# A gated recurrence rebuilt from seven block products instead of eight, in blocks of 512 positions

## The chip, the cores and the metric

One core of a Trainium2 chip runs the kernel. The core has a matrix engine (PE, whose weight loads the profile lists as PEld), a vector engine (DVE), a scalar engine (ACT), a general one (POOL), and a queue that issues transfers (SP). They run side by side and wait for each other through semaphores. SBUF is the on-chip memory that all of them read; PSUM holds the sums of PE in eight banks of 128 partitions by 512 float32 columns; DRAM is reached by transfers. The metric is the time of one execution in microseconds. Three executions of the kernel before took 2949.99, 2952.07 and 2953.89 us, so the median is 2952.07.

## The reference

The input r has 8 sequences of 2048 positions and 512 channels. Two layers follow one another, each with a normalisation before it, a normalisation of its result and a residual sum:

```
x = r
x = x + layernorm(gelu(longconv(layernorm(x))))          # a state-space convolution along the 2048 positions
n = layernorm(x)
for the 8 steps t (the batch axis is the time of this layer; the 2048 positions are its batch):
    f = sigmoid(n[t] @ wf.T + c @ uf.T + bf)
    i = sigmoid(n[t] @ wi.T + c @ ui.T + bi)
    g = tanh   (n[t] @ wc.T + c @ uc.T + bc)
    c = f * c + i * g                                    # c starts from in_c in every position
h = tanh(n @ wo.T + c_final @ uo.T + bo)                 # n[t] for each t, c_final once
x = x + layernorm(h)
```

All the 512 x 512 matrices and all rows of n and c are float32. The kernel splits each operand into a float16 value and a float16 remainder and adds three float16 products, so each product of the reference is three on PE.

## The kernel before

The first stage computes the convolution kernel and the statistics of the input rows. The second stage is the convolution itself, in 16 groups of 32 channels (loop over `g`, lines 601 to 659, `NG` = 16). Within a group, 16 slots (`s_`) each issue matmuls for this group (`conv_mm`), the state chain of the next group (`chain_hi`, `chain_lo`, `chain_in`, `tap_step`), and the normalisation of the group after that (`norm_x`). The last group is `conv_last` (line 545): it first finishes the first `JF` = 2 blocks of 128 positions, so that the next stage can begin, and then the others. The result goes to DRAM as `y_d`. The gate weights are loaded and split into halves during groups 1, 2, 13 and 14 and stay in SBUF.

The third stage is the gated recurrence, over eight blocks (`q`) of 256 positions and eight steps `t`. For each (q, t):

- `prep` (line 687) loads rows of `y_d` and of r, normalises (`lnstat`: DVE's statistics, POOL's power -1/2), adds, and writes x1 to DRAM for the end; `norm` normalises again; `turn` (line 712) transposes on PE and splits into halves `xt`. These run two steps ahead (`AHEAD`).
- `scan` (line 725) takes four output blocks `m` of 128 channels. For each it issues 3 gates x 4 input blocks x 3 products of 128x128 by 128x256 for x, and as many for the state `ch` where t > 0, into PSUM tiles `pfi` and `pgg`. ACT applies tanh (line 744), DVE forms the new state (lines 750 to 754), ACT and DVE split it (755, 756).
- `head` (line 776) computes the x part of the output for the block before (q-1), 24 products with 512 columns, adds the state's part `uo` (from `last`, line 766), applies tanh, normalises and adds x1, which it reads back. Its last sum is on POOL (line 792). The heads of the last block come after all scans.

The order on PE, ACT, DVE and POOL is the order of the program text in the stretches under `manual_schedule`, and a scheduler's elsewhere; the order on SP is always the scheduler's. A tile pool with `bufs=n` hands the same memory out again when its earlier user is done, and the wait for that is inserted for the new user. The helper `mm3` (line 386) issues the three products; in the profile all products that go through it have its lines 388 to 390 and are told apart by their tiles.

## Time and profile before

The profiled execution took 2954.2 us; its span, from the first to the last instruction, is 2952.4 us.

| | us |
|---|---|
| median of three executions | 2952.07 |
| profiled execution | 2954.2 |
| its span | 2952.4 |
| PE busy | 2828.6 |
| DVE busy | 1670.6 |
| ACT busy | 1017.7 |
| POOL busy | 718.5 |
| last product of the convolution starts | 610.1 |
| first product of the recurrence starts | 616.5 |
| last gate product of the recurrence starts | 2891.1 |
| mean granted clock of PE | 0.979 |

A group line of the page names the line, engine and operation, the tile written and those read, the shape, the count, and after the bar the busy time in all, the mean of one in ns, and the idle time of the engine just before, with what ended most of it. A line of the busy time by stretch gives, after the window and its length, PE, PEld, DVE, ACT and POOL with their instruction counts, then PE's granted clock (1.00 is full), the share of the transfer engines and the rate in GB/s. A timeline line gives the start, the duration, the engine, the line and the operation. Matmuls overlap: a product of 256 columns is shown with 0.27 us, but the starts of neighbours show the pace.

### The profile page before, as it was taken

To read this page: it belongs to the slowest core of one execution; us is meant where nothing else is said; L and a number is where in the kernel's file an instruction comes from. 1 tells how busy PE (TensorE), PEld (TensorE's weight loads), DVE (VectorE), ACT (ScalarE), POOL (GpSimd) and SP (SyncE) were. 2 spreads that over 40 slices of the span, in tenths; PEclk is the share of its full clock that TensorE was granted. 3 is DMA by queue.
4 is the path that set the end of the run, shared out by engine and by line. 5 is a ranking of instruction groups with operands and counts; after the bars stand their busy time and mean duration, and the time that the engine had idled before them with its cause. 6 is when DMAs were issued, how large, how long until landed. Compare 5 with 4: busy or idle time off the path is not lost.

```text
span 2952.4 us, 59431 instructions
## 1 busy us (share of the span) xinstructions
PE 2828.6 (96%) x25044; PEld 2353.3 (80%) x25044; DVE 1670.6 (57%) x3674; ACT 1017.7 (34%) x2288; POOL 718.5 (24%) x723
## 2 busy tenths in 40 slices
PE   4679999899999999999999999999999999999998
PEld 3368888798888888888788878887888888888884
DVE  8867777647445555555555565555555655553336
ACT  8856666623222222222222222222222222222222
POOL 5757877301001111111111111111111211110003
PEclk8689999989999999999999999999999999999999
DMA  6867777747222222222222232223222322221002
GB/s 236 291 206 230 227 228 233 206 110 158 73 58 72 72 72 72 72 72 72 72 72 72 72 80 70 69 70 86 72 72 72 80 69 72 70 78 44 30 30 104
DMA packets 459476, 311.32 MB, mean 105 GB/s; under 512 B 282310, under 2 KB 377032, under 8 KB 455112
## 3 DMA queue, kind: packets, MB, share of 16 engines
q1 hardware_dynamic: 458776, 306.99, 37.4%
q8 instruction: 196, 3.21, 0.5%
q14 instruction: 72, 0.59, 0.1%
q10 hardware_dynamic: 432, 0.52, 0.1%
HBM read 206.28 MB, written 101.19 MB: 104 GB/s over the span
## 4 chain that ended last, share of the span: by engine, by line
PE 74%; issue 10%; DVE 4%; DMA 3%; POOL 3%; ACT 1%; POOLq 0%; SPq 0%; DVEq 0%; ACTq 0%
PE pfi L390 12%; PE pfi L389 12%; PE pfi L388 12%; PE pgg L389 6%; PE pgg L388 6%; PE pgg L390 6%; PE pz L390 3%; PE pz L389 3%; PE pz L388 3%; PE pt L721 2%; PE pyt L389 2%; PE pyt L390 2%; PE pyt L388 1%; DVE xg L467 1%; DMA wl<-in_wt 1%
## 5 line engine op out<-in xcount | busy, mean ns | idle before, releaser
L389 PEld LDWEIGHTS <-w 128*128 128x128 f16 x5808 | 568.1, 98 | 73.2 <-issue 6.4
L388 PEld LDWEIGHTS <-w 128*128 128x128 f16 x5808 | 568.1, 98 | 72.1 <-issue 0.7
L390 PEld LDWEIGHTS <-w 128*128 128x128 f16 x5808 | 568.0, 98 | 72.0
L388 PE MATMUL pfi<-xt,w 128*128 128x256 f16 x2048 | 559.8, 273 | 0.7 <-ACT xt L83 0.7
L389 PE MATMUL pfi<-xt,w 128*128 128x256 f16 x2048 | 560.0, 273 | 0.0
L390 PE MATMUL pfi<-xt,w 128*128 128x256 f16 x2048 | 559.8, 273 | 0.1
L388 PE MATMUL pfi<-ch,w 128*128 128x256 f16 x1792 | 488.6, 273 | 5.1 <-ACT ch L755 5.1
L390 PE MATMUL pfi<-ch,w 128*128 128x256 f16 x1792 | 488.6, 273 | 0.1
L389 PE MATMUL pfi<-ch,w 128*128 128x256 f16 x1792 | 488.6, 273 | 0.0
L744 ACT ACTIVATE gate<-pfi,bias 128x256 f32<-128x256 f32 x512 | 214.6, 470 | 656.2 <-PE pfi L390 655.7
L750 DVE SCALAR_TENSOR_TENSOR a<-gate,cd 128x256 f32<-128x256 f32 x224 | 114.9, 513 | 514.6 <-ACT gate L744 514.6
L680 POOL TENSOR_TENSOR rsh<-rsh,nhalf 128x2 f32<-128x2 f32 (+1 forms) x65 | 45.1, 694 | 1465.3 <-DVE rsh L679 1442.0
L755 ACT ACTIVATE ch<-cd 128x256 f16<-128x256 f32 x256 | 106.5, 416 | 516.5 <-DVE cd L754 516.5
L388 PE MATMUL pgg<-xt,w 128*128 128x256 f16 x1024 | 279.3, 273 | 0.0
L389 PE MATMUL pgg<-xt,w 128*128 128x256 f16 x1024 | 279.2, 273 | 0.0
L390 PE MATMUL pgg<-xt,w 128*128 128x256 f16 x1024 | 279.1, 273 | 0.0
L388 PE MATMUL pgg<-ch,w 128*128 128x256 f16 x896 | 244.4, 273 | 0.0
L389 PE MATMUL pgg<-ch,w 128*128 128x256 f16 x896 | 244.4, 273 | 0.0
L390 PE MATMUL pgg<-ch,w 128*128 128x256 f16 x896 | 244.2, 273 | 0.0
L792 POOL TENSOR_TENSOR x1r<-x1r,h 128x512 f32<-128x512 f32 x124 | 182.2, 1488 | 41.1 <-DVE h L791 41.1
L753 DVE SCALAR_TENSOR_TENSOR gate<-gate,gate 128x256 f32<-128x256 f32 x256 | 110.6, 432 | 136.8 <-ACT gate L744 136.8
L83 ACT ACTIVATE xt<-pt 128x512 f16<-128x512 f32 x128 | 75.8, 596 | 316.3 <-PE pz L390 218.3
(301 smaller groups left out, 5786.6 us busy)
## 6 DMA issues: line engine op xcount, KB each, us to landing
xs<-in_rr SPq DMA_DIRECT2D x32, 1024.0 KB, 7.1
t<-kpad SPq DMA_DIRECT2D x32, 1024.0 KB, 5.3
xr<-in_r SPq DMA_DIRECT2D x128, 256.0 KB, 3.4
x_d<-x SPq DMA_DIRECT2D x128, 256.0 KB, 3.4
x1r<-x_d SPq DMA_DIRECT2D x128, 256.0 KB, 3.2
out<-x1r SPq DMA_DIRECT2D x128, 256.0 KB, 2.0
y<-y_d SPq DMA_DIRECT2D x62, 512.0 KB, 5.5
y_d<-y SPq DMA_DIRECT2D x30, 1024.0 KB, 7.7
```

The lines of the kernel that those rows point to most:

```text
L83: S.activation(hi, src, AF.Copy)
L388: T.matmul(out, lhsT=w(0), rhs=x(0), start=start, stop=False)
L389: T.matmul(out, lhsT=w(1), rhs=x(0), start=False, stop=False)
L390: T.matmul(out, lhsT=w(0), rhs=x(1), start=False, stop=stop)
L467: V.tensor_tensor(xg, xg, bc(rs1), ALU.mult)
L680: Q.tensor_tensor(rs, rs, nhalf[:, 0:n], ALU.pow)
L721: T.transpose(pt[:, k], xn[:, k * P : (k + 1) * P], ident)
L744: S.activation(r, outs[gt], AF.Tanh, scale=gsc[gt], bias=bs[:, gt, m : m + 1])
L750: V.scalar_tensor_tensor(a2, gate[0], 1.0, cst_[q, t - 1, m], ALU.add, ALU.mult)
L753: V.scalar_tensor_tensor(gate[1], gate[1], 1.0, gate[2], ALU.add, ALU.mult)
L755: S.activation(ch[:, 0], cd, AF.Copy, scale=0.5)
L792: (V if (q, t) >= (NQB - 1, NB - 2) else Q).tensor_tensor(x1r, x1r, hv[cj], ALU.add)
```

## The change

Each 512 x 512 product is cut into 2 x 2 blocks of 256 and formed by seven block products instead of eight, with sums of blocks taken on both operands beforehand and of results afterwards. The block of positions grows from 256 to 512 (`QC` = 4 blocks of 128), so there are four blocks `q` and 32 steps (q, t).

- **Weights.** For each of seven matrices the four blocks give seven operands (three plain, four sums), in two halves each; they are formed during groups 1 to 14 of the convolution (`weight_pieces`) and kept in DRAM as `wf_d`, then loaded whole (`weights`): two matrices at group 14, one at group 15, four when the convolution is over. The first state's part of the bias is formed on DVE from `in_c` and the untransposed matrices (`first_piece`) instead of by 144 one-column products.
- **Rows.** `prep` takes two steps t at a time and writes x1 to DRAM; `turn` reads x1 back, normalises, transposes and forms the seven operands `xf`. Scaling a row (`scaled`) moves from DVE to ACT, with the negative mean formed on POOL.
- **Products.** A unit is a gate and a half `n` of its channels, or for the x part of the output ("z") a half of the positions; its sums lie in a PSUM tile `u` of four columns blocks (two banks), of which three exist. `part_x` issues four of the seven products for x, `part_c` those for the state; then ACT copies one block, DVE adds it to the others inside PSUM (line 879), and `part_b` lets the other three products add to these sums. Each step has two z units and six gate units, interleaved by hand.
- **State.** `state` forms the new state for half of the channels and its seven operands `cf`.
- **Output.** The x part goes to DRAM as `z_d`, the state's part as `u_d`, and `head` reads both back, one row block at a time, for the block before; the last 32 row blocks follow at the end. `JF` becomes 4.

```diff
-JF = 2
+JF = 4
+QC = 4
+FIRST = (((FA11, FB11, UX), (FS2, FT2, UY)), ((FS1, FT1, UV), (FS3, FT3, UZ)))
+THEN = ((FA12, FB21, UX), (FN22, FT4, UZ), (FS4, FB22, UV))
...
+    def first_piece(gt, m):
+        un = FJ.tile([P, H], F32, name="un")
+        dma(out=un, in_=a["un"][gt, m])
+        V.scalar_tensor_tensor(un, un, 1.0, c0r, ALU.mult, ALU.mult, accum_out=puc[:, gt, m : m + 1])
...
+        for n, job in enumerate(jobs):
+            if n < NG - 3:
+                at(n + 1, 0 if n == 0 else -1, job[0])
+                for s_, f in zip(JS, job[1:]):
+                    at(n + 1, s_, f)
...
+    def scaled(out, x, mu, rs):
+        nm = FE.tile([P, 1], F32, name="nm", bufs=4)
+        Q.tensor_tensor(nm, mu, rs, ALU.mult)
+        Q.tensor_scalar(nm, nm, -1.0, None, ALU.mult)
+        S.activation(out, x, AF.Identity, scale=rs, bias=nm)
+
+    def prep(q, tp, cj):
...
+            xr = xas[k] = FJ.tile([P, 2, H], F32, name="xr", tag="wl")
...
+        def sum_():
+            y, xr = ytile.pop(k), xas.pop(k)
+            for t, (mu, rs) in enumerate(xas.pop((k, 0))):
+                yv, xv = y[:, :, t], xr[:, t].rearrange("p (g h) -> p g h", h=HS)
+                scaled(yv, yv, mu, rs)
+                Q.tensor_tensor(xv, yv, xv, ALU.add)
+            dma(out=x1_d[c, :, 2 * tp : 2 * tp + 2], in_=xr)
...
+    def turn(q, t, i):
...
+        def norm():
+            for x, (mu, rs) in zip(xas[k], xas.pop((k, 0))):
+                scaled(x, x, mu, rs)
+        def split_():
...
+            S.activation(b1, pt[:, :, 0:2], AF.Copy)
+            V.tensor_tensor(ts[:, 0:2], pt[:, 1].rearrange("p (a k) c -> p a k c", a=2), b1, ALU.subtract)
+            V.tensor_tensor(ts[:, 2], pt[:, 1, 2:4], ts[:, 0], ALU.subtract)
+            V.tensor_tensor(ts[:, 3], ts[:, 2], pt[:, 0, 2:4], ALU.subtract)
+            for f, src in (...):
+                split(xf[:, f, 0, :, cs], xf[:, f, 1, :, cs], src)
...
+    def part_x(key):
+        u = units[key] = pu.tile([P, 4, BP], F32, name="u")
+        for pr in FIRST:
+            mms(u, places(key, pr), *views(key)[0], True, not key[1] or key[2] == "z")
+
+    def part_c(key):
...
+        if t and not z:
+            mms(u, FIRST[0][:1] + FIRST[1] + FIRST[0][1:], *views(key)[1], False, True)
+        if z:
+            g = zts[key] = FJ.tile([P, 4, BP], F32, name="zt", tag="ws")
...
+        S.activation(u2, u[:, UX], AF.Copy)
+        V.tensor_tensor(u2, u2, u[:, UY], ALU.add)
+        V.tensor_tensor(c22, u2, u[:, z_], ALU.add)
+        V.tensor_tensor(c22, c22, u[:, v_], ALU.add)
+        V.tensor_tensor(u[:, 2:4], u[:, 2:4], u2[:, None].to_broadcast([P, 2, BP]), ALU.add)
+        if not z:
+            S.activation(c22, c22, AF.Tanh, ...)
+
+    def part_b(key):
...
+        mms(u, places(key, THEN), *wx, False, z or not t)
+        if z:
+            zt = zts.pop(key)
+            S.activation(zt[:, 0], u[:, UX], AF.Copy)
+            S.activation(zt[:, 1:3], u[:, 2:4], AF.Copy)
+            for h in range(2):
+                dma(out=z_d[QC * q + n + 2 * h, :, t], in_=zt[:, 2 * h : 2 * h + 2].rearrange("p a b -> p (a b)"))
+            return
+        if t:
+            mms(u, THEN, *wc, False, True)
...
+        act(g[:, 0:2], u[:, 0:3:2], bs[:, n : n + 1])
+        act(g[:, 3], u[:, UZ], bs[:, n + 2 : n + 3])
+        if kind == 2:
+            V.scalar_tensor_tensor(g, gates.pop((q, t, 1, n)), 1.0, g, ALU.add, ALU.mult)
+        elif kind == 0:
+            state(q, t, n)
...
+    def head(q, cj, t0, tail=False):
...
+        def sum_():
+            (V if tail else Q).tensor_tensor(z, z, us_[c], ALU.add)
+        def gate():
+            S.activation(heads[k], heads[k], AF.Tanh, scale=1.0 / SW)
+        def stat():
+            x1r = FT.tile([P, H], F32, name="x1r", bufs=2)
+            dma(out=x1r, in_=x1_d[c, :, t0])
+            heads[k, 0] = lnstat([heads[k]], "h") + [x1r]
+        def out():
+            z, ((mu, rs), x1r) = heads.pop(k), heads.pop((k, 0))
+            scaled(z, z, mu, rs)
+            Q.tensor_tensor(x1r, x1r, z, ALU.add)
+            dma(out=a["out"][c, :, t0], in_=x1r)
...
+            keys = [(q, t, "z", 0), (q, t, "z", 1)] + [(q, t, gt, mp) for mp in range(2) for gt in (1, 2, 0)]
+            for sl, key in enumerate(keys):
+                part_x(key)
+                if sl == 3:
+                    part_b(before)
+                    before = keys[2]
+                part_c(key)
+                go(*side.get(2 * sl, ()))
+                if before and sl != 2:
+                    part_b(before)
+                if sl != 2:
+                    before = key
+                go(*side.get(2 * sl + 1, ()))
+        part_b(before)
+        go(*last(NQB - 1))
+        rows = [head(NQB - 1, cj, t, True) for cj in range(QC) for t in range(NB)]
+        D = (0, 1, 1, 1, 2)
+        for n in range(len(rows) + max(D)):
+            for st_, d in sorted(enumerate(D), key=lambda v: -v[1]):
+                if 0 <= n - d < len(rows):
+                    rows[n - d][st_]()
```

The pieces of `prep`, `turn`, `head` and `last` are put between the units by hand, at sixteen places (`side`, two to a unit): a step with heads has two preps, two turns (for the step that follows) and four head rows.

## The prediction

> **What bounds the kernel now.** Read first the busy shares and the 40 slices of the page, then the busy time by stretch, then the costliest groups with shapes kept apart, PE's timeline and the waits.
>
> ```profile
> PE 2828.6 (96%) x25044; PEld 2353.3 (80%) x25044; DVE 1670.6 (57%) x3674; ACT 1017.7 (34%) x2288; POOL 718.5 (24%) x723
> PE   4679999899999999999999999999999999999998
> DVE  8867777647445555555555565555555655553336
> ```
> ```profile
> 184.00:548.00 364.00, 344.80 (x4008) 303.95 (x4008) 270.16 (x453) 247.71 (x552) 282.90 (x232) 0.99 0.75 225
> 588.00:592.00 4.00, 4.00 (x68) 4.00 (x67) 0.72 (x5) 0.47 (x1) 0.00 (x0) 0.52 0.95 271
> 700.00:2800.00 2100.00, 2094.50 (x17759) 1745.51 (x17758) 1110.47 (x2479) 539.80 (x1164) 284.41 (x276) 1.00 0.28 72
> ```
> ```profile
> 1199.73 0.27 PE L388 MATMUL pgg<-xt,w 128*128 128x256 f16 x1
> 1199.84 0.27 PE L389 MATMUL pgg<-xt,w 128*128 128x256 f16 x1
> 1199.95 0.27 PE L390 MATMUL pgg<-xt,w 128*128 128x256 f16 x1
> ```
> ```profile
> 1203.22 0.42 ACT L755 ACTIVATE ch<-cd 128x256 f16<-128x256 f32 x1 [5.37 <-DVE cd L754]
> 1204.21 0.84 ACT L744 ACTIVATE gate<-pfi,bias 128x256 f32<-128x256 f32 x2 [0.58 <-PE pfi L390]
> ```
> ```profile
> L744 ACT ACTIVATE gate<-pfi,bias 128x256 f32<-128x256 f32 x512 | 214.6, 470 | 656.2 <-PE pfi L390 655.7
> L792 POOL TENSOR_TENSOR x1r<-x1r,h 128x512 f32<-128x512 f32 x124 | 182.2, 1488 | 41.1 <-DVE h L791 41.1
> L753 DVE SCALAR_TENSOR_TENSOR gate<-gate,gate 128x256 f32<-128x256 f32 x256 | 110.6, 432 | 136.8 <-ACT gate L744 136.8
> ...
> L83 ACT ACTIVATE xt<-pt 128x512 f16<-128x512 f32 x128 | 75.8, 596 | 316.3 <-PE pz L390 218.3
> ```
> ```profile
> x1r<-x_d SPq DMA_DIRECT2D x128, 256.0 KB, 3.2
> out<-x1r SPq DMA_DIRECT2D x128, 256.0 KB, 2.0
> ```
>
> The second line of the page shows PE at nine tenths from slice 5 to the end. In the stretches the columns are the five engines' busy time, PE's clock, the DMA share and GB/s. From 700 to 2800 us PE is busy 2094.5 of 2100; its waits there total 5.3. Matmuls start every 0.109 us: PE's count of products is the time. ACT, DVE and POOL stand waiting (ACT 656 us for PE), so their round trips cost nothing now.
>
> **The change, part by part.**
>
> *PE, saved.* Before, 512 positions at t>0 take 2 x 288 products at 0.109, 2 x 24 of 512 columns (0.216 apart in the last heads) and 16 transposes (four in 0.60): 62.8+10.4+2.4 = 75.6. After: 6 gates x 84 + 2 x 42 for the x part = 588 products, 64.1, plus 2.4: 66.5. At t=0: 44.2 before, 39.0 after. 28 x 9.1 + 4 x 5.2 = 276 us saved; the same-shaped output product of the last state gets 60 products of 512 columns per 512 positions for 48, +2.6, four times. If the other engines kept up, that would be the gain.
>
> *Side engines, added.* Per step of 512 positions (`part_x`, `part_c`, `part_b` for two z units and six gate units) they now also combine PSUM blocks, split seven operand sums, copy z, reread z and x1. ACT, DVE and POOL run in the order written by hand, so a wait for another engine holds all behind it. `scaled` is the link: POOL makes `nm` in two tiny operations, ACT scales, POOL adds, and the next row's `nm` stands behind that add.
>
> I walk one step with heads (q>=1, t>0) from the end of ACT's tanh of the unit before the last. Rows used: ACT 256 columns 0.38 copy and 0.47 tanh, 512 columns 0.60 to 0.69, 1024 1.06; DVE 256 0.42, 512 0.69, 1024 1.28, statistics of two rows 1.7; POOL add 1.45, power 0.7; a hand-over 0.04. `nm` has no row: between the 0.20 of a POOL copy of 128x5 and the 0.55 of the one-column power; I take 0.25, nearest to the copy. ACT's clock:
> - 9.0: u2 of z0, the last gate's tanh, `state` on DVE with its four copies.
> - 18.4: u2 of z1. `zt` has one buffer, so DVE's c22 of z1 waits for z0's write: copies end at 10.3, landing 2.0 to 3.4 later, I take 13.5. Behind it: z1's sums, prep's statistics (1.7), the first gate's four DVE operations, its tanh.
> - 25.9: prep's two rows and turn's two, the link at full length: scale to 19.0, POOL's add 20.6, `nm` 21.1, scale 21.8, add 23.3, power 24.1, `nm` 24.6, scale 25.3, scale 25.9. ACT works 2.5 of these 7.5 us.
> - 33.5: z1's copies, u2, DVE's sums, heads a and b (an add between them), tanh.
> - 36.8: turn's split, ACT and DVE in turns.
> - 47.4: two gates; between them DVE's 1024-column product, two statistics (3.4), sums.
> - 54.1: prep, turn again. 60.4: tanh and `state` of the first half.
> - 68.0: u2, tanh, heads' statistics, second split. 71.3: heads c and d. 74.6: last gate.
>
> PE needs 66.5 of that 74.6. Operations back to back go at a shorter pitch (two of 0.47 in 0.84 above), so I take 73 (66.5 to 79). Without heads (q=0) about 7 go: 67 (66.5 to 70). PE's places of waiting: the x products of the third gate (third `u` buffer, freed by z1's copies at 26.9) and the last gate's second half (DVE sums at the end of the step).
>
> t=0: PE needs 39, but the side work is that of other steps, plus `last` (13.0 of PE, four DVE additions through one buffer) or, at q=0, four preps: 75 (55 to 85) and 70 (60 to 80).
>
> *Lead-in.* Before: last convolution product 610.2, first scan product 616.5. After: the first rows go statistics, scale, add, DRAM, back, statistics, scale, transpose, split, twice, the second pair behind the first; `xr` has one buffer, so a row pair is loaded only after the one before has landed. Four weight loads of 1.8 MB stand before these writes on SP's queue: 7.3 MB at 271 to 291 GB/s, 26 us. By rows: weights landed 640; second pair's add 647, landed 650, back 653, split 662; second half 693. The step then runs as if begun at 685: 75 after the convolution (40 to 110).
>
> *Convolution.* Groups of 28 us gain about 4.8 us of DVE, 2.1 of ACT and 1.7 MB; DVE is at 74%, DMA at 0.75 and 225 GB/s, which becomes about 286 where the busiest slice has 291. Hidden by those gaps, or 14 x 5 us if gone: 20 (0 to 70). The 4.8 us are four sums of 256 columns (0.42 each), products of 512, 256 and 1024 (0.69, 0.42, 1.28) and one of 512 for the first state's bias; ACT's are 0.60, 0.40 and 1.06. The last group's first part takes four blocks instead of two: as many products, same time; the cover is PE's own work. 144 one-column products (5 us) go; they lie in the lead-in.
>
> *Tail.* Before, 61 us from the last scan product (2891) to the end, PE working on heads. After, 32 rows remain, PE done. First state, `last`, u through DRAM: 28 us. Then per row the loop: `nm` twice, scale 0.63, tanh 0.63, statistics 1.1, power 0.55, hand-overs: 3.6 (x1r's two buffers: write 2.0, load 2 to 3.2, add 1.4, over two, 3.5). 28 + 32 x 3.6 + 5 = 148 (133 to 165).
>
> *Sum* against the profiled run, 2954.2 us (span 2952.4; 2.1 above the median of the three runs, 2952.07): 610 + 20 + 75; q=0 70 + 7 x 67 = 539; q=1..3 3 x (75 + 7 x 73) = 1758; last half unit 3; tail 148; 2 around the span: 3155, so 3153 on the median's scale, 6.8% slower.
>
> **A rule weighed.** The rows: at 588 to 592 the clock stands at 0.52 with PE busy throughout, after a stretch of waits. The Trainium skill, TensorE: Matmul & The Clock Gate, "The HAM clock gate (the 'warmup' mystery)", says that an idle window of about 3.4 us halves the clock until a busy one passes. My walk has two PE waits near 3.7 us per step; by the rule each could cost up to 1.7 us of PE time, an estimate from that page of 71 us over 21 steps if PE were last, giving 3224. By the rows I leave it out: in the groups of 28 us PE waits too and the clock is 0.99.
>
> **Rivals.**
> (a) *PE stays last in every step* (the other side): the waits of ACT fall into time that PE fills. For: ACT is busy only 26% in the scan. Against: it is not its busy time but its hand-overs that add up. Every step at 66.5, t=0 at 55 to 60: with my lead-in and tail 2946; with their low ends and no loss in the convolution 2876. It decides only where a step with heads takes under 65 us with my other terms (2954 = 612+20+75+539+24p+151), which is below PE's own 66.5, so lead-in and tail must shrink too.
> (b) *Worse*: SP's queue holds loads behind writes that wait, or the clock halves: steps of 79, lead-in 110, convolution 70, high ends all through: 3300 to 3444. For: each step issues some 30 transfers on SP, many of them waiting for POOL; against: most have ten us and more of lead.
> (c) *The products do not get cheaper*: 0.124 apart instead of 0.109, the weight load (98 ns in the rows, hidden) coming out. PE then needs 75 per step, more than the side walk: 21 steps of 75 to 76 for 73 and seven of 75 for 67, 3250. It can be told from the forecast only in the profile. Against: shape and operands are the same as now.
>
> **How the numbers follow.** Forecast (3060 to 3260) 0.64; (a) 0.15, of it 0.08 faster, 0.01 same, 0.06 slower; (b) 0.18; (c) 0.03. Within 0.2% is about what a measurement of this kernel can't tell from no change. Faster 0.08, same 0.01, slower 0.91. The range 2970 to 3330 leaves out the better part of (a) and the worse part of (b), some 2 in 10.
>
> **What would show it.** Right: PE's slices at 8 and 9 from q=1 on, steps with heads near 73 us by the pitch of `z_d` writes and near 67 before; ACT's idle before L766 put down to POOL, DVE's before L877 to a DMA; a hole of some 75 us after the convolution; a tail of about 148 us with PE at 0. Wrong: steps at 66.5 throughout, or row tails far from 3.6 us.

## The result, and the profile of the changed kernel

The changed kernel takes 3450.43 us (median of four runs, 3449.84 to 3452.41) where the kernel before takes 2951.03 (2949.48 to 2953.89) on the same chip: 1.169 times as long, 95% interval 1.167 to 1.171. The profiled run has a span of 3448.0 us. The direction and the chief mechanism, engines that wait for each other in their fixed orders, are as forecast; the size is not: it is 297 us more than the 3153 forecast, 120 above the upper end of the range.

The stages, in us of the profiled run, beside the terms of the prediction's sum:

| stage | predicted | measured |
|---|---|---|
| up to the last convolution product | 610 + 20 | 655 |
| lead-in | 75 | 92 |
| q=0: first step, seven others | 70, 7 x 67 | 82, 7 x 74.9 |
| q=1 to 3: first step, seven others | 75, 7 x 73 | 93.4, 7 x 78.7 |
| last half unit and tail | 3 + 148 | 162 |

The steps are counted from one first write of `z_d` to the next; the tail starts at the last gate product (3286.0), and the lead-in is what is left of the span. Of q=3's seven, the last ones (t=5 and t=6, and t=7 within the rest) have no rows left to prepare and take 66.1 to 66.2; the 18 steps that have both head rows and preparation take 80.8 on average.

From the page of the changed kernel, busy shares, PE's 40 slices and the clock that PE was granted:

```profile
PE 2726.7 (79%) x23940; PEld 2298.1 (67%) x23940; DVE 2073.9 (60%) x4254; ACT 1499.4 (43%) x3020; POOL 1167.7 (34%) x1782
PE   4688888437999898788888877888888788889920
PEclk8799999668999999899999999999999899999965
```

PE is at 96% no longer. There is a hole after the convolution (the 4 and 3) and an empty end, and in between PE is at 7 to 9 tenths; no other engine is full either. Who waits for whom stands in the groups from 700 to 3280 us (busy us and mean ns, then idle time before them and its releaser):

```profile
L837 PE MATMUL u<-xf,w 128*128 128x256 f16 x8046 | 1018.3, 286 | 247.0 <-DVE u L879 232.9 <-ACT gate L900 7.0 <-DVE u__30505 L960 2.5
L766 ACT ACTIVATE y<-y,nm,rsy 128x512 f32<-128x512 f32 x124 | 99.9, 806 | 128.7 <-POOL nm L765 124.4 <-DVE mvy L753 4.3
L766 ACT ACTIVATE xa<-xa,nm,rsx 128x512 f32<-128x512 f32 x128 | 97.2, 806 | 160.3 <-POOL nm L765 160.3
L766 ACT ACTIVATE zr<-zr,nm,rsh 128x512 f32<-128x512 f32 x96 | 77.5, 807 | 110.1 <-POOL nm L765 110.1
L823 DVE TENSOR_TENSOR ts<-pt,b 128x512 f32<-128x512 f32 x64 | 44.0, 688 | 184.3 <-DMA z_d<-zt 155.9 <-ACT b L822 28.4
L877 DVE TENSOR_TENSOR zt<-u2p,u 128x256 f32<-128x256 f32 x64 | 26.9, 421 | 95.5 <-DMA z_d<-zt 83.8 <-ACT u2p L875 10.6
```

PE waits for DVE's block sums (L879), ACT for POOL's `nm`, DVE for writes of `z_d`: a ring of engines, each waiting in its order of instructions. Before the change PE had 5.3 us of waits in 2100. Two steps with heads and preparation, and one that has no preparation left, as stretches (us; then busy time and count of PE, PEld, DVE, ACT, POOL; PE's clock, DMA share, GB/s):

```profile
1783.20:1863.90 80.70, 71.75 (x607) 61.06 (x605) 48.84 (x101) 32.95 (x63) 25.01 (x44) 0.94 0.40 108
1863.90:1946.30 82.40, 71.82 (x606) 61.32 (x604) 48.71 (x101) 32.93 (x63) 24.96 (x44) 0.94 0.38 103
3099.50:3165.60 66.10, 66.08 (x606) 59.18 (x604) 45.28 (x91) 29.97 (x59) 16.94 (x30) 1.00 0.26 85
```

The third line is what the change would give if nothing but PE counted: 606 instructions in 66.1 us. The other two carry as many, take 15 to 16 us more, and PE is even busy 5.7 us longer with them: its clock is 0.94.

### The profile page after: what moved, and what is told of

The parts are those of the page before. It is cut to its first block, busy times and chain, and to the rows that moved or that the text cites. A ratio compares the mean times of both kernels' runs of the same rounds, so it can differ in the third digit from the quotient of the medians.

```text
span 3448.0 us, 60459 instructions
## 1 busy us (share of the span) xinstructions
PE 2726.7 (79%) x23940; PEld 2298.1 (67%) x23940; DVE 2073.9 (60%) x4254; ACT 1499.4 (43%) x3020; POOL 1167.7 (34%) x1782
## 4 chain that ended last, share of the span: by engine, by line
DVE 34%; ACT 16%; PE 15%; POOL 12%; DMA 11%; issue 7%; SPq 0%; POOLq 0%; ACTq 0%; DVEq 0%
PE u L837 9%; DMA z_d<-zt 6%; POOL xr L788 5%; ACT xf L101 3%; ACT y L766 3%; DVE xf L102 3%; DVE cd L920 2%; POOL x1r L991 2%; DVE gate L877 2%; DVE gate L878 2%; ACT gate L900 2%; DVE u L879 2%; DVE u2p L876 2%; ACT zr L766 2%; DVE gate L919 2%
## 5 line engine op out<-in xcount | busy, mean ns | idle before, releaser
L837 PEld LDWEIGHTS <-w 128*128 128x128 f16 x15120 | 1518.6, 101 | 497.0 <-DVE u L879 258.4
L837 PE MATMUL u<-xf,w 128*128 128x256 f16 x8064 | 1020.5, 286 | 247.1 <-DVE u L879 232.9
L837 PE MATMUL u<-cf,w 128*128 128x256 f16 x7056 | 840.6, 276 | 0.0
L837 PE MATMUL u<-w,xf 128*128 128x256 f16 x2688 | 324.6, 280 | 35.4 <-DVE u L879 26.1
L837 PEld LDWEIGHTS <-xf 128*128 128x128 f16 x2688 | 269.0, 100 | 78.3 <-DVE u L879 15.3
L900 ACT ACTIVATE gate<-u,bias 128x512 f32<-128x512 f32 (+1 forms) x384 | 198.6, 567 | 127.7 <-PE u L837 127.6
L991 POOL TENSOR_TENSOR x1r<-x1r,zr 128x512 f32<-128x512 f32 x128 | 169.5, 1325 | 237.0 <-ACT zr L766 237.0
L788 POOL TENSOR_TENSOR xr<-y,xr 128x512 f32<-128x512 f32 x128 | 164.1, 1282 | 180.7 <-ACT y L766 151.6
L879 DVE TENSOR_TENSOR u<-u,u2p 128x512 f32<-128x512 f32 x256 | 179.0, 699 | 8.8
L527 POOL TENSOR_TENSOR xg<-xg,mu 128x512 f32<-128x512 f32 x112 | 162.9, 1461 | 9.4 <-DMA xg<-in_xr 9.4
```

What stands on the lines that cost most here:

```text
L527: Q.tensor_tensor(xg, xg, bc(mu1), ALU.subtract)
L788: Q.tensor_tensor(xv, yv, xv, ALU.add)
L837: T.matmul(u[:, d], lhsT=w(f, b, i == 1, k), rhs=x(f, b, i == 2, k), start=opens and bank not in seen, stop=stop and j == len(n) - 1, skip ...
L879: V.tensor_tensor(u[:, 2:4], u[:, 2:4], u2[:, None].to_broadcast([P, 2, BP]), ALU.add)
L900: act = lambda o, s_, b: S.activation(o, s_, AF.Tanh, scale=gsc[kind], bias=b)
L991: Q.tensor_tensor(x1r, x1r, z, ALU.add)
```

## The experiments

Times are medians. Each run was made beside the kernel before on the same chip (2949.8 to 2953.2 us), and the ratios are to that; where a run is set against the changed kernel, that is 3450.43. Two runs set against each other may have been on different chips, which moves a difference by up to 3 us.

**Theory**: the pace of a step is a ring of hand-overs between ACT, DVE and POOL, each in order, whose links are the single `zt` buffer and `nm`. **Rivals**: PE itself, at a lower clock, sets the pace; or only one of the two links does, and covers the other.

### A second tile for z

```diff
         if z:
-            g = zts[key] = FJ.tile([P, 4, BP], F32, name="zt", tag="ws")
+            g = zts[key] = (FE.tile([P, 4, BP], F32, name="zt", tag="y", bufs=2) if n else FJ.tile([P, 4, BP], F32, name="zt", tag="ws"))
```

> Edit: z1's tile of combined x-part sums gets the spare buffer of y, so it no longer waits for z0's write, and turn's operand sums no longer wait for z1's write. Theory A (a chain of hand-overs between ACT, DVE and POOL sets the pace, and these two waits, 3.0 and 5.4 us of DVE per step, are links of it): steps with heads from 81 to between 73 and 78 us, steps at q=0 from 75 to between 67 and 71, the whole 3215 to 3340 us. Theory B (PE itself or its clock sets the pace): steps stay at 80 to 82, 3440 to 3455 us. Theory C (POOL's nm alone is the chain and DVE's waits lie beside it): steps fall by less than 2 us, 3400 to 3450.

3321.64 us, ratio 1.125 (1.1233 to 1.1267): 129 less than the changed kernel. Steps with heads take 77.4 us for 80.8, at q=0 68.6 for 74.9. Both are within theory A's numbers; the waits of L823 and L877 for `z_d` are gone.

### `nm` with the statistics

```diff
     def lnstat(src, tag):
...
         Q.tensor_tensor(rs, rs, nhalf[:, 0:n], ALU.pow)
-        return [(mv[:, i, 0:1], rs[:, i : i + 1]) for i in range(n)]
+        nm = FE.tile([P, n], F32, name="nm" + tag, bufs=2)
+        Q.tensor_tensor(nm, mv[:, :, 0], rs, ALU.mult)
+        Q.tensor_scalar(nm, nm, -1.0, None, ALU.mult)
+        return [(nm[:, i : i + 1], rs[:, i : i + 1]) for i in range(n)]
...
-    def scaled(out, x, mu, rs):
-        nm = FE.tile([P, 1], F32, name="nm", bufs=4)
-        Q.tensor_tensor(nm, mu, rs, ALU.mult)
-        Q.tensor_scalar(nm, nm, -1.0, None, ALU.mult)
+    def scaled(out, x, nm, rs):
         S.activation(out, x, AF.Identity, scale=rs, bias=nm)
```

> Edit: nm is worked out with the statistics, for both rows at once, so that no nm stands behind another row's POOL add. Theory A (hand-over chain, POOL's adds a link): about 1.7 us of ACT's waiting goes at each of four places in a step with heads and at two in a step of q=0; steps with heads from 81 to 74 to 78, q=0 from 75 to 71 to 74, tail rows from 4.2 to about 3.8; the whole 3280 to 3390 us. Theory B (PE or its clock): 3440 to 3455. Theory C (DVE's waits for the z write are the chain, and POOL's waits lie beside them): steps fall by less than 2 us, 3400 to 3450.

3227.93 us, ratio 1.0941 (1.0923 to 1.0959): 222 less, a larger gain than theory A's range (3280 to 3390) has. Steps with heads take 72.0 us, at q=0 69.9. The tail's rows did not move (4.19 us): there the order is one row's addition, the next row's power and `nm`, and moving `nm` within that loop takes nothing out of it.

### Both

Both edits in one kernel.

> Both edits, the second buffer and nm with the statistics. Theory A: the gains add until PE's own 66.5 is reached: steps with heads 66.5 to 71, q=0 66.5 to 68, the whole 3100 to 3230 us, and PE's waits for DVE's sums nearly gone. Theory B (PE at a lower clock): steps stay over 75. Theory C (one of the two waits covers the other): no more than the better of the two alone.

3064.02 us, ratio 1.0376 (1.0361 to 1.0392): 386 less than the changed kernel, more than 129 + 222, and below theory A's lower end of 3100. Two steps with heads of this kernel, as stretches, and the two groups of DVE and one of ACT:

```profile
1955.00:2020.90 65.90, 65.90 (x605) 59.05 (x603) 48.63 (x101) 32.91 (x64) 24.10 (x37) 1.00 0.46 129
2035.20:2101.20 66.00, 66.00 (x607) 59.34 (x606) 48.46 (x101) 32.64 (x64) 23.76 (x36) 1.00 0.48 133
```
```profile
L766 ACT ACTIVATE zr<-zr,nmh,rsh 128x512 f32<-128x512 f32 x96 | 72.8, 802 | 18.0 <-POOL nmh L759 18.0
L823 DVE TENSOR_TENSOR ts<-pt,b 128x512 f32<-128x512 f32 x64 | 44.0, 688 | 86.9 <-ACT b L822 86.9
L877 DVE TENSOR_TENSOR zt<-u2p,u 128x256 f32<-128x256 f32 x64 | 27.0, 421 | 4.2 <-issue 0.4
```

The steps stand at 65.9, PE is busy throughout and its clock is 1.00, while DVE has as much work as in the changed kernel (48.6 us a step for 48.8). So neither DVE's nor ACT's amount of work set the pace of the steps; the two links did. PE's work is the same in all; its lower clock went away with the waits, so it is a consequence of them. The means over the 18 steps with heads and preparation, from the traces, in us:

| kernel | step | PE busy | PE waiting |
|---|---|---|---|
| changed | 80.8 | 70.7 | 10.1 |
| second tile | 77.4 | 69.9 | 7.5 |
| `nm` moved | 72.0 | 67.7 | 4.3 |
| both | 66.1 | 66.0 | 0.1 |

### The scale back on DVE

On top of the second tile for z.

```diff
     def scaled(out, x, mu, rs):
-        nm = FE.tile([P, 1], F32, name="nm", bufs=4)
-        Q.tensor_tensor(nm, mu, rs, ALU.mult)
-        Q.tensor_scalar(nm, nm, -1.0, None, ALU.mult)
-        S.activation(out, x, AF.Identity, scale=rs, bias=nm)
+        V.tensor_scalar(out, x, mu, rs, ALU.subtract, ALU.mult)
```

> Undoes one part of the change: rows are scaled by one DVE operation with mean and rstd, as before the change, and nm and ACT's scale go; beside it z1's tile is the spare buffer of y (3322 us without the undoing). Theory A (the link was the route over POOL and ACT, not the amount of work): 12 operations of 0.54 to 0.90 us more on DVE per step fit, steps with heads fall from 77.5 to between 66 and 70 us, the whole 3050 to 3140 us. Theory B (DVE, which also carries the block sums, becomes the pace): steps stay at 74 or more, the whole 3220 to 3330.

3040.76 us, ratio 1.0306 (1.0292 to 1.032), 23 less than with the second tile and `nm` moved (3064.02). Steps stand at 65.9 with DVE at 56.7 of them. The route over POOL and ACT relieved an engine that had room and put a link into the ring; with it out, the kernel takes 281 us less than with the second tile alone (3321.64).

### The convolution: places, work or transfers

Groups of the convolution take 31.8 us where they took 27.9. First the weight work at other places of a group, then without the work, then without the transfers.

```diff
-                at(n + 1, 0 if n == 0 else -1, job[0])
-                for s_, f in zip(JS, job[1:]):
+                if n == 0:
+                    at(1, 0, job[0])
+                for s_, f in zip((13, 14, 15), job[1:]):
                     at(n + 1, s_, f)
+                at(n + 2, 0, job[4])
                 if n + 1 < NG - 3:
-                    at(n + 1, 9, jobs[n + 1][0])
+                    at(n + 2, 0, jobs[n + 1][0])
...
-            at(n + 1, 14, lambda gt=gt, m=m: first_piece(gt, m))
+            at(n + 1, 12, lambda gt=gt, m=m: first_piece(gt, m))
```

`JS` was (2, 5, 8, 12).

> Edit: in the convolution the weight pieces move from the places 2, 5, 8, 12 and 14 of a group to 12 to 15 and 0, where no or few tap splits stand before them on DVE; work and transfers are the same. Theory A (PE waits since pieces, tap splits and norms come in bursts ahead of the chain's split on DVE): groups of 31.8 us become 28 to 30, the whole 20 to 50 us shorter, 3400 to 3430. Theory B (DVE or the transfers are short of throughput over the whole group): groups stay within 0.8 us of 31.8, the whole 3435 to 3465.

3485.24 us, ratio 1.1803 (1.1785 to 1.182): 35 slower, which neither theory had. Groups take 34.1 us. From 200 to 550 us:

```profile
L547 PE MATMUL pxt<-x,at 128*128 128x256 f16 x288 | 59.4, 291 | 35.6 <-ACT x L101 35.6
L553 PE MATMUL pxt<-x,at 128*128 128x256 f16 x144 | 41.8, 290 | 12.7 <-DVE x L102 12.7
L392 ACT ACTIVATE wq<-ws 128x1024 f16<-128x1024 f32 x10 | 10.6, 1057 | 22.2 <-DVE ws L409 22.2
```

PE's waits for DVE did fall, from 44.8 to 12.7 us, but ACT now stood waiting in front of a weight copy for DVE's sums, with the chain's copy queued behind it: ten waits of PE for ACT, of up to 3.7 us, one in each group, where no wait had been over 1.6. PE's waits in all hardly grew, from 44.8 to 48.3 us. What grew is PE's own time, as the stretch from 200 to 550 us shows, of the changed kernel and then of this run:

```profile
200.00:550.00 350.00, 302.31 (x3462) 262.44 (x3460) 280.44 (x485) 232.57 (x507) 245.73 (x199) 1.00 0.81 252
```
```profile
200.00:550.00 350.00, 301.02 (x3254) 261.03 (x3253) 280.37 (x455) 214.64 (x470) 217.88 (x187) 0.91 0.76 233
```

PE is busy as long with 208 products fewer, at a clock of 0.91 for 1.00. Of the 2.3 us that a group became longer, PE's busy time is about 1.9.

```diff
             else:
                 ws = wjob["s", w, i]
-                V.tensor_tensor(ws[:, 1], ws[:, 0], a11, ALU.subtract)
-                V.tensor_tensor(ws[:, 3], a12, ws[:, 1], ALU.subtract)
...
-            wr = FJ.tile([P, 3, 2, BP], F16, name="wr")
-            halves((wr[:, 0:2, 0], wr[:, 0:2, 1]), wl[:, :, 0:BP], sc)
-            halves((wr[:, 2, 0], wr[:, 2, 1]), wl[:, 1, BP:], -sc)
+            wr = wjob["wr"]
             dma(out=wf_d[WORDER.index(w), :, i, 0:3], in_=wr)
```

The same is done to the rest of `sums`, to `summed`, `first_piece` and the output's weights; `wjob["wr"]` is a constant tile.

> Leaves out (of the changed kernel, 3450 us) ACT's and DVE's weight work in the convolution; loads and writes of the same size stay, so weights and first state are wrong. Theory A (work: DVE's pieces stand ahead of the chain's split): groups of 31.8 us become 27.9 to 29, PE's waits for DVE's split fall to a third, the whole 3395 to 3415. Theory B (transfers: 1.7 MB more per group on queues already at 0.75): groups stay within 0.8 of 31.8, the whole 3440 to 3455.

```diff
-            wl = wjob[w, i] = FJ.tile([P, 2, H], F32, name="wl")
-            dma(out=wl, in_=a["wt"][w].rearrange("(a k) p m -> p k a m", a=2)[:, i])
+            if "wl" not in wjob:
+                wjob["wl"] = FJ.tile([P, 2, H], F32, name="wl")
+                dma(out=wjob["wl"], in_=a["wt"][w].rearrange("(a k) p m -> p k a m", a=2)[:, i])
+            wjob[w, i] = wjob["wl"]
...
-            dma(out=wf_d[WORDER.index(w), :, i, 0:3], in_=wr)
+            if w == 0:
+                dma(out=wf_d[0, :, i, 0:3], in_=wr)
```

> Leaves out (of the changed kernel, 3450 us) the weight transfers in the convolution except those of the first matrix; ACT's and DVE's weight work stays, on the first matrix over and over, so the weights are wrong. Theory A (work): groups stay within 0.8 of 31.8, the whole 3440 to 3455. Theory B (transfers): groups of 27.9 to 29, the whole 3395 to 3415. Between the two if both have a part.

Without the work: 3418.45 us, ratio 1.1584 (1.1567 to 1.1602). Without the transfers: 3442.63, ratio 1.1668 (1.165 to 1.1685). The stretch from 340 to 550 us, in a fence each, of the kernel before, of the changed kernel, without the work and without the transfers:

```profile
340.00:550.00 210.00, 201.69 (x2373) 178.38 (x2372) 154.44 (x262) 143.38 (x322) 161.36 (x135) 1.00 0.73 220
```
```profile
340.00:550.00 210.00, 180.69 (x2077) 156.79 (x2075) 168.31 (x293) 139.92 (x308) 147.29 (x121) 1.00 0.81 253
```
```profile
340.00:550.00 210.00, 201.71 (x2367) 178.05 (x2366) 154.48 (x271) 143.46 (x322) 162.23 (x134) 1.00 0.74 225
```
```profile
340.00:550.00 210.00, 180.68 (x2077) 156.90 (x2076) 168.06 (x293) 139.97 (x307) 147.44 (x120) 1.00 0.67 203
```

Without the work PE has the 201.7 us of the kernel before again (2367 products for 2373) and groups of 27.9; without the transfers, at 50 GB/s less, nothing changes. It is the work of DVE and ACT, which of the two was not separated. The total without the work falls by only 32 us, 3 short of theory A's range: in that run PE stood once, at 208 to 238 us, for 29.8 us, which was not looked into.

### The lead-in

On top of both edits of the steps; `wrote` and `got` list the writes of the preps and the loads of the turns.

```diff
-            xr = xas[k] = FJ.tile([P, 2, H], F32, name="xr", tag="wl")
+            xr = xas[k] = FJ.tile([P, 2, H], F32, name="xr", tag=("wl", "wq", "ws", "wl")[cj] if q == tp == 0 else "wl")
...
             for cj in (i, i + 2):
                 go(*prep(0, 0, cj))
+        for i in range(2):
             go(*turn(0, 0, i))
-    for w in WORDER[3:]:
-        weights(w)
+    with tc.issue_after(wrote[1].ins):
+        weights(3)
+    with tc.issue_after(got[3].ins):
+        for w in (4, 5, 6):
+            weights(w)
```

> Edit, on top of both edits of the steps (3064 us): the first three row pairs get tiles of their own for xr, all four preps stand before the first turn, the weights of x's product are loaded after the second row pair's write and those of the recurrence after turn's last load. Theory A (the hole after the convolution is made by SP's queue: 7.3 MB of weights ahead of the first rows, and row pairs that wait for the one xr tile): first z0 write 35 to 50 us earlier than at 750.6, the whole 3012 to 3032 us. Theory B (it is the chain of the rows itself, statistics, scale, DRAM and back, twice): first z0 write less than 15 us earlier, the whole over 3048.

3028.64 us, ratio 1.0264 (1.0247 to 1.0281): 35 less than with both edits of the steps, the first write of `z_d` at 713.6 for 750.6 (2.4 of the 37 stand before, at the convolution's end): theory A's numbers. Rows of SP's queue from 655 to 700 us, of the changed kernel and then of this one (start, time on SP; others left out):

```profile
658.52 2.31 SPq L611 DMA_DIRECT2D w<-wf_d  x4
...
670.90 0.32 SPq L789 DMA_DIRECT2D x_d<-xr  x1
...
684.42 0.98 SPq L777 DMA_DIRECT2D xr<-in_r  x1
685.46 0.45 SPq L801 DMA_DIRECT2D xa<-x_d  x1
```
```profile
663.70 0.32 SPq L790 DMA_DIRECT2D x_d<-xr  x1
...
666.96 1.38 SPq L778 DMA_DIRECT2D xr<-in_r  x1
668.40 0.46 SPq L802 DMA_DIRECT2D xa<-x_d  x1
```

In the first, the write of 670.9 stands behind four weight loads, and the next rows' load, which needs the same tile, goes out 13.5 us after it; in the second 3.3 us. The edit has three parts (tiles of their own, the order of preps and turns, the weights later), which were not tried one by one.

### The tail

On top of both edits of the steps: rows loaded ahead into tiles that the scan has left, `u` kept in tiles, one row between statistics and last addition.

```diff
-            z = heads[k] = FT.tile([P, H], F32, name="zr", bufs=3)
+            if tail:
+                n = cj * NB + t0
+                z = heads[k] = FT.tile([P, H], F32, name="zr", **(dict(bufs=3) if n % 6 < 3 else dict(tag=("w3", "w4", "w5")[n % 6 - 3])))
+                x1r = heads[k, 1] = FT.tile([P, H], F32, name="x1r", **(dict(bufs=2) if n % 6 < 2 else dict(tag=("w6", "gate0", "gate1", "cd1")[n % 6 - 2])))
...
-        D = (0, 1, 1, 1, 2)
+        D = (0, 4, 4, 5, 6)
```

> Edit, on top of both edits of the steps (3064 us): in the tail, rows are loaded four rows ahead into tiles that the scan has left (6 each for z and x1), statistics and the last addition are one row apart each, and u stays in its tiles. Theory A (the row's loop is one of hand-overs through few buffers): rows every 2.6 to 3.2 us for 4.2, the tail 112 to 135 us from the last gate product for some 169, the whole 3010 to 3032 us. Theory B (POOL's work or the transfers of 0.75 MB a row set the rows): rows stay over 3.9, the whole over 3050.

3039.1 us, ratio 1.0298 (1.0283 to 1.0314): 25 less, rows every 3.52 us for 4.19. That is between the two theories. Buffers or the order of a row's parts were part of it (the edit changes both); what is left is ACT's scale waiting 2.19 us a row for the `nm` of POOL, which stands behind POOL's addition of the row before.

### Together, in four forms

The first: both edits of the steps, the lead-in, the tail with `D = (0, 2, 2, 3, 5)`, and in the convolution the sums on POOL, the rest in five pieces.

```diff
-                V.tensor_tensor(ws[:, 0], a21, wl[:, 1, BP:], ALU.add)
+                Q.tensor_tensor(ws[:, 0], a21, wl[:, 1, BP:], ALU.add)
...
+                for s_, f in zip((6, 9, 13, 14, 15), job[1:]):
                     at(n + 1, s_, f)
+                at(n + 2, 0, job[6])
```

> Both edits of the steps, the lead-in's, the tail's with statistics and the last addition two rows apart, and in the convolution the four sums on POOL and the rest of the weight work in five pieces of at most 0.7 us, four of them at places without tap splits. Theory A (DVE's bursts ahead of the chain's split, and the hand-over loop of a row): groups of 31.8 us become 28.5 to 30.5, rows of 3.5 us 2.4 to 2.9, the whole 2915 to 2955 us. Theory B (POOL's norm chain has no room for the sums, rows are set by the transfers): groups 31 or more, rows 3.2 or more, the whole 2980 to 3010.

3006.71 us, ratio 1.0193 (1.0179 to 1.0207). Rows 3.26 us, groups 32.4: theory B's numbers in both. In the tail its cause is another than the transfers that B named: a row's tanh waits for DVE's addition, which stands behind the statistics of the row before, and that addition takes 1.41 us for 0.68 (the last section has the rows). The head rows of t=0 moved to the steps t=1 to 4:

```diff
-                for i in range(4):
-                    r = 4 * t + i
+                HN = (0, 5, 5, 5, 5, 4, 4, 4)
+                for i in range(HN[t]):
+                    r = sum(HN[:t]) + i
```

> As the run before it, and the four head rows of each step t=0 go to the steps t=1 to 4 (five rows each). Theory A (t=0, where PE has 54 us of work in 82, is set by the hand-over chain, and the steps at 65.9 have room on the other engines): t=0 falls by 6 to 12 us, the others stay within 0.5, the whole 18 to 36 us less than the run before it. Theory B (t=0 is set by state and sums, or a fifth row breaks the cover in t=1 to 4): less than 8 us, or slower.

3018.03 us, ratio 1.023 (1.0216 to 1.0244): t=0 falls from 82 to 71.5 us, as theory A has it, but the steps of five rows rise from 65.9 to between 68.4 and 71.6: theory B, and the whole is 11 us slower: the rows cost more where they go than where they were. Next, all weight work on DVE and ACT in seven pieces, the scale on DVE, and in the tail no addition on POOL:

```diff
+            if tail:
+                S.activation(x1r, x1r, AF.Identity, bias=mu)
+                V.scalar_tensor_tensor(x1r, z, rs, x1r, ALU.mult, ALU.add)
...
+                for s_, f in zip((13, 14, 15), job[1:]):
                     at(n + 1, s_, f)
+                for s_, f in zip((1, 2, 3), job[4:]):
+                    at(n + 2, s_, f)
```

> The lead-in's edit, the one-operation scale on DVE and z1's tile beside y; in the tail POOL does only the power and nm, ACT adds nm to x1 and DVE scales and adds in one operation; in the convolution all weight work stays on DVE and ACT, in seven pieces of at most 0.85 us at the places 13, 14, 15, 0, 1, 2, 3, where tap splits are short or absent. Theory A (in the run before, DVE's operations were stretched by POOL's beside them, and bursts did the rest): groups of 32 us become 28.5 to 30.5, rows of 3.3 us 2.4 to 2.8, the whole 2915 to 2950 us. Theory B (DVE is short over the whole group, whatever the places): groups 31 to 32.5, rows as in A, the whole 2955 to 2985.

3005.78 us, ratio 1.0182 (1.0168 to 1.0197): above both theories' ranges. Groups take 31.6 us, theory B's number, with DVE busy 181.9 of the 210 us from 340 to 550 (168.3 in the changed kernel). That DVE is short over the whole group, wherever the pieces stand, is argued from this and not shown: PE still has a wait of 2.3 us in each group, and its clock there is 0.95. Rows take 3.80 us, more than with POOL's addition, which neither theory had; the chain of ACT and DVE in this tail shows why (this kernel's timeline, ACT and then DVE):

```profile
2940.84 0.63 ACT L1004 ACTIVATE zr<-zr 128x512 f32<-128x512 f32 x1 [2.55 <-DVE zr L1001]
2941.37 0.70 ACT L1017 ACTIVATE x1r<-x1r,nmh 128x512 f32<-128x512 f32 x1
```
```profile
2940.06 0.68 DVE L1001 TENSOR_TENSOR zr<-zr,u__36134 128x512 f32<-128x512 f32 x1
2942.11 0.75 DVE L1018 SCALAR_TENSOR_TENSOR x1r<-zr,rsh,x1r 128x512 f32<-128x512 f32 x1 [1.37 <-ACT x1r L1017]
```

DVE's last product waits for ACT's addition, which stands behind the tanh of a later row, which waits for DVE's first addition: a ring again, made by the order alone. The same with the heads of t=0 moved, the fifth row early in its step:

```diff
-                    p = ((8, 10, 11, 12, 13), (8, 10, 11, 12, 13), (13, 14, 15, 15, 15), (13, 14, 15, 15, 15)) if t == 0 else (
-                        (0, 2, 3, 5, 6), (0, 2, 3, 5, 6), (6, 8, 9, 12, 13), (6, 8, 9, 12, 13))
+                p = [(0, 2, 3, 5, 6), (0, 2, 3, 5, 6)] + [(0, 3, 4, 7, 8)] * (HN[t] == 5) + [(6, 8, 9, 12, 13)] * 2
```

> As the run before it, and the head rows of t=0 go to the steps t=1 to 4, the fifth row early in the step. Theory A (with the shorter chain those steps have room for a fifth row): t=0 falls by 8 to 12 us, the steps t=1 to 4 stay under 67, the whole 15 to 35 us less than the run before it. Theory B (DVE's work, 2.2 us a row, comes before a gate's sums again): steps of five rows 68 us or more, the whole within 10 us of the run before it or slower.

3020.03 us, ratio 1.0232 (1.0217 to 1.0246): theory B once more, steps of five rows 67 to 72 us, the whole 14 us slower.

No version beats the kernel before; the nearest is 1.8% behind. By the first of the four (3002.1 us for 2952.4, profiled): convolution 51 us longer, lead-in 45, tail 70, and the scan 116 shorter, 2159 for 2275.

## Why the prediction was right or wrong

*PE, saved*: right. 66.5 was worked out per 512 positions; steps in which nothing else holds take 66.1 to 66.2, and once the links are out all steps from t=1 on take 64.8 to 66.6.

*Side engines, added*: right that they set the pace and that `nm` and the write of `z_d` are links, wrong in size; this is the first step that failed. One wait was missing, one was too short, and PE's slower products after its waits were left out. The forecast took 73 us for a step with heads, from a walk of 74.6, and the steps with preparation take 80.8. In the step that starts at 1850.4 us, the stretches of ACT's clock, predicted and measured: 9.0 and 12.6; 9.4 and 10.7; 7.5 and 7.5; 7.6 and 7.2; 3.3 and 6.1; 10.6 and 10.3; 6.7 and 6.7; 6.3 and 6.2; 7.6 and 9.3; 3.3 and 3.7; 3.3 and 3.2. Seven of eleven are within half a microsecond, the two with POOL's link (7.5, 6.7) exact, and four (the first, second, fifth and ninth) carry the whole difference. In two of these DVE waits for the write of `z_d`:

```profile
1868.78 0.42 DVE L877 TENSOR_TENSOR zt<-u2p,u 128x256 f32<-128x256 f32 x1 [4.64 <-DMA z_d<-zt]
...
1890.26 0.69 DVE L823 TENSOR_TENSOR ts<-pt,b 128x512 f32<-128x512 f32 x1 [5.84 <-DMA z_d<-zt]
```

The first was in the walk, but with 3.2 us from z0's copies to the landed write where it was 4.9. The second was missing: `turn`'s sums use the tag of `zt` too and wait for z1's write. In the other two, PE is slow after having waited (the last row is the next step's):

```profile
1849.76 4.02 PE L837 MATMUL u<-xf,w 128*128 128x256 f16 x18 [4.01 <-DVE u L879]
...
1870.44 2.12 PE L837 MATMUL u<-w,xf 128*128 128x256 f16 x18 [1.48 <-DVE u L879]
...
1882.10 4.45 PE L837 MATMUL u<-xf,w 128*128 128x256 f16 x24
...
1920.77 3.45 PE L837 MATMUL u<-xf,w 128*128 128x256 f16 x18 [2.78 <-DVE u L879]
...
1933.17 3.52 PE L837 MATMUL u<-xf,w 128*128 128x256 f16 x18 [4.37 <-DVE u L879]
```

Eighteen products take 2.1 us after a wait of 1.5, as long as without one, but 3.5 to 4.0 after waits of 2.8 to 4.4. The length of the wait alone does not decide it: the 24 products at 1882.10 follow a wait of 1.5 us and eight transposes, and take 4.45 us where 2.78 is usual. They cost nothing on ACT's clock; the stretch around them took 7.2 us for 7.6. The discount from 74.6 to 73, for operations back to back, has nothing in the measured stretches to support it.

*q=0 and t=0*: that some 7 us go without heads was nearly right (80.8 to 74.9, so 5.9); the rest is the error above, carried along: 55 us over seven steps. t=0 took 82 and 93.4 for 70 and 75. With the links out it still takes 82 (q=1 to 3), of which PE stands about 17 waiting for DVE's block sums (L879) in the first of them; its head rows are 10 us of the 82, and cost 15 in the four steps that take them instead. What orders the rest was not taken apart, so this part of the miss (12 and three times 18 us) has no shown cause.

*A rule weighed*: the second step that failed. The rule was left out, because the clock in the convolution was 0.99 with waits there. Those waits are at most 1.6 us long; the steps' are longer, and 606 products took 71.8 us of PE where they take 66.1 without waits. The same convolution with a wait of 3.7 us in each group has a clock of 0.91. The row that the prediction quotes, 588 to 592 us, is no clean case for it: the last wait before it ended at 581.5, and PE is busy when the clock falls at 588. The Trainium skill (TensorE: Matmul & The Clock Gate, "The HAM clock gate") states that the clock halves after an idle window of about 3.4 us; the rows here agree in kind, though a wait of 2.78 us was already enough. The 5.7 us a step are PE's; how much of them lay on the path, rather than in waits that others filled, is only argued from the first and the ninth stretch of the walk.

*Convolution*: 45 for 20 us, within its range; the term that failed was that the pieces mostly hide in the gaps of DVE, ACT and the transfers. They do not: PE waits about 4 us a group, and the run without the work gets them back, the run without transfers does not. Three other arrangements of the work (34.1, 32.4 and 31.6 us a group) did not hide it either.

*Lead-in*: 92 for 75, within its range. Up to the second pair's addition it went as forecast (34 us after the convolution for 37); the second pair's half then took 40 us for 31. The lead-in run showed that the order on SP, the one tile and the order of the pieces make 35 us of it in the kernel with both edits of the steps, which the walk had as given.

*Tail*: 162 for 151, of it the rows 4.19 for 3.6: `scaled` 0.81 for 0.63, and the power 0.96 for 0.55 (in the steps it takes 0.57). The rest of the tail took 28 us for 36, so the miss of the rows is in part hidden.

*Sum*: 25 + 17 + 67 + 175 + 11 us over the stages, 295 in all. *Rivals*: (a) was excluded by the steps, but names what the kernel does once both links are out. (b) came nearest with 3444, in part by luck: its steps of 79 are near the measured 78.7, but its convolution (70 for 45) and lead-in (110 for 92) are too long and make up for its t=0 (85 for 93.4) and its steps of q=0 (70 for 74.9), which are too short; it took the clock for a cause beside the chain, where it was the chain's consequence, and SP's queue mattered in the lead-in only. (c) is excluded by 65.9.

## What to carry to other kernels

Where engines run in a fixed order, look for tiles that share a buffer, and for tiny operations that stand behind large ones: a second tile and a reordering of two 0.2-us operations took 386 us off this kernel with each engine's work nearly the same. Write down every tag that a tile shares before walking a step, since the wait that was missed here was a tag's. And a saving on the one full engine is worth its full size only where the others stay out of its way; here PE's saving was paid back before and after the scan, where it has nothing to do.

## What the runs showed of the hardware

PE's clock falls to half for some microseconds after longer waits. The changed kernel, at the wait of 4.01 us and at the products of 1882.10:

```profile
1848.40:1855.20 6.80, 5.45 (x26) 3.89 (x27) 4.89 (x8) 1.72 (x4) 2.77 (x3) 0.50 0.57 172
1882.50:1885.90 3.40, 3.40 (x18) 2.37 (x17) 1.81 (x4) 1.21 (x2) 0.89 (x1) 0.50 1.27 216
```

In the convolution, waits of up to 1.6 us left the clock at 1.00, one of 2.3 us a group went with 0.95, one of 3.7 with 0.91. Waits are not the whole rule: the kernel before shows 0.50 from 588.1 to 601.8 us with PE busy all of the time:

```profile
588.10:601.80 13.70, 13.70 (x195) 13.70 (x195) 0.79 (x4) 2.23 (x4) 0.00 (x0) 0.50 0.51 139
```

So a link in a ring can cost PE twice, by the wait and by the slower products after it. In the 18 steps of the table above, the two edits alone remove 3.4 and 8.8 us, together 14.7; of the 2.5 us above their sum, PE's busy time is 0.8 and its waits are the rest. By this count the clock makes up only a part of what the two edits gain beyond their sum; the rest is not explained.

DVE and POOL slow each other. In the tail of the first combined kernel, DVE's addition of two tiles in SBUF runs beside POOL's addition, in that of the third POOL does no addition (a fence each):

```profile
2948.61 1.41 DVE L998 TENSOR_TENSOR zr<-zr,u__36806 128x512 f32<-128x512 f32 x1
2951.86 1.41 DVE L998 TENSOR_TENSOR zr<-zr,u__36806 128x512 f32<-128x512 f32 x1
```
```profile
2940.06 0.68 DVE L1001 TENSOR_TENSOR zr<-zr,u__36134 128x512 f32<-128x512 f32 x1
2943.85 0.68 DVE L1001 TENSOR_TENSOR zr<-zr,u__36134 128x512 f32<-128x512 f32 x1
```

1.41 us for 0.68, same operation, same size; POOL's addition takes 1.26 us there as in the changed kernel's tail. The other way round, POOL's power of 128x1 takes 0.94 to 1.02 us in the tails where it starts beside DVE's addition, and 0.57 in the steps. The Trainium skill (GPSIMD Engine Reference, "8. Key points") states that POOL shares its SBUF interfaces with DVE and contends with DVE instructions that have two inputs in SBUF; these rows agree. It may be why the four sums moved to POOL brought nothing in the convolution; no run took that apart.

ACT's time for 128x512 goes with what it reads beside the tile: 0.63 us for the tanh with neither column, 0.70 for the sum with a bias column, 0.81 for the scaling with a bias and a scale column. The tanh with a bias column, which reads PSUM, takes 0.67 us.
